# One fused layer on one core: block 0's first u ahead of h_1's moments, fd_hi casts and x differences moved, one output's scaling split in two

## The chip, the cores and the metric

One core of one Trainium2 chip runs the whole program. The metric is device time in microseconds; lower is better. The engines are PE (matrix products; PEld is its weight load), DVE (vector), ACT (scalar activations), POOL (GpSimd) and SP (which here issues transfers). Each engine runs its own instructions one after the other; semaphores tie the engines together.

## The reference

A batch of 4 x 2048 tokens of 256 features passes an attention-like layer without softmax, and then a gated feed-forward layer with integer weights. Both are followed by a layer norm without weights.

```python
Q, K, V = x @ W_q.T, x @ W_k.T, x @ W_v.T          # 256 features
mask = where(i >= j, decay ** (i - j), 0)          # inside chunks of 32 tokens
O = (Q K^T * mask) V                               # chunk by chunk
a = (sigmoid(x @ W_g.T) * O) @ W_o.T + x
h = layernorm(x + a)
f = (silu(h @ wg.T) * (h @ wu.T)) @ wd.T           # 768 hidden, int weights / 127
out = layernorm(h + f)
```

## The kernel before

The 8192 tokens are cut into 16 blocks of 512 (TB). Each block passes an attention stage and a feed-forward stage; the loop over b (0 to 13, from L1088 on) does the feed-forward stage of block b, the scores and values of block n = b + 2, and the token projections (gate, y, v) of block m = b + 3, with their products interleaved on PE. Blocks 0 and 1 have their attention in a prologue ahead of the loop, and blocks 14 and 15 have their feed-forward stage behind it. The iteration b = 13 is the last attention block: there is no block m (the name `more` is false), and its feed-forward products stand alone beside the scores and the output projection of block 15.

Precision comes from splitting operands. A token tile x becomes x_hi (ACT, scaled by TOP), x_lo (POOL, the rest) and x_gap (DVE, a difference made by `gaps()` in `token_parts`, L473); the weights likewise. A projection is then three products in `three` (L520): hi by hi and lo by lo first, then ACT multiplies the bank by WHOLE in place (L527), then gap by gap is added to the same bank, and `finish` takes it away. So PE cannot start the gap products (p_v, p_y, p_g, p_o) before ACT has scaled that bank. The hidden values u are split into u_hi (fp32r, ACT, L898) and u_lo (f16, POOL, L899), h into hT_hi and hT_lo.

`ffn_up` makes one chunk of 128 hidden features: 16 products into the banks fg and fu, s = silu(fg) on ACT (L882), u = fu * s on DVE (L893), then u_hi on ACT and u_lo on POOL. With `held=True` the part from u on is handed back as `multiply`, to be called after other work has been put between. There are six chunks, 0 to 5, for each block. The down projection (`project_back`, or the chunkwise form in `ffn_down` for b = 13) needs all u_hi and u_lo of a block; the chunkwise form does the terms of chunks 0 to 3 first, then the p_o gap products of block 15, then the rest.

The weights fg, fu and fd come as int32 tiles. `integers` (L272) hands back a function that casts one of the two forms, hi or lo, in three pieces on ACT (L282). For fd, the hi form is cast at b = 0 behind `look_up(range(4, n_pieces))`, which takes maxima of the integer tiles on DVE; the lo form is cast between s and u of chunks 4 and 5 of b = 0 by `up_with_cast`.

The layer norm of h takes its mean and variance with bn_stats and bn_aggr on DVE (`moments`, L332 and L333, eight instructions a block). Most blocks take the root on ACT; h_0, h_1, the last h and the last outputs use a chain on POOL (`iterated_scale_and_shift`: a power at L408, then short steps). `normalize` applies scale and shift with four ACT instructions (L420). From block 1 on h goes through `move_h`: four 32x32 transposes on DVE (sq), then 16 transfers on the SP queue (hT), then the split into hT_hi (ACT) and hT_lo (POOL). Outputs are normalized by the same `normalize` one iteration later and stored from SP.

What sets the order: the code writes it out by hand. `in_turn` and `in_steady_turn` pin an instruction behind everything traced on its engine before it. Instructions without it, such as those of the POOL chain, may be placed earlier by the scheduler when their inputs are ready. In the prologue, before the change, the order around h_1 is:

```python
    x_parts, x_gaps = token_parts(xTs[3], "x_3")
    scales_h = iterated_scale_and_shift(out_rest(), of_h, "h_1")
    x_gaps()
    ahead = yT, v, sg
```

`out_rest()` issues the p_o gap products of block 1, the two additions that make h_1 (L784), and the moments. Chunk 0 of block 0 comes after all of that, as the first thing in the loop.

Of the kernel before, what the change touches and what calls it, by code (L numbers as in the profile page):

```python
# [59 lines left out]
NG = TB // P  # L60
# [16 lines left out]
def kernel(  # L77
# [249 lines left out]
    def moments(r, name, groups=range(NG), order=free, mv=None):  # L327

        mv = no_moments(name) if mv is None else mv
        for g in groups:  # L330
            st = small.tile([P, 6], F32, tag="st", name=f"st_{name}_{g}")
            order(nc.vector.bn_stats(st, r[:, g, :]))  # L332
            order(nc.vector.bn_aggr(mv[:, g, :], st))  # L333
        return mv
# [33 lines left out]
    of_h, of_out = (HALF, H_UP), (H_UP, 1.0)  # L368
# [19 lines left out]
    def iterated_scale_and_shift(mv, kind, name):  # L388
        on_r, on_dst = kind

        def column(tag):
            return small.tile([P, NG], F32, tag=tag, bufs=2, name=f"{tag}_{name}")

        def times(out, a, b):
            nc.gpsimd.tensor_tensor(out, a, b, ALU.mult)

        def line(out, a, slope, at_0):
            nc.gpsimd.tensor_scalar(out, a, slope, at_0, ALU.mult, ALU.add)

        v, y, t, minus, shift = map(  # L400
            column, ("v", "y", "t", "minus_mean", "term")
        )
        in_turn(
            nc.vector.tensor_scalar(
                v, mv[:, :, 1], 1 / on_dst**2, EPS * (on_r / on_dst) ** 2, ALU.mult, ALU.add
            )
        )
        nc.gpsimd.tensor_tensor(y, v, half, ALU.pow)  # L408
        nc.gpsimd.tensor_scalar(minus, mv[:, :, 0], -1.0, None, ALU.mult)
        times(t, y, y)  # L410
        times(t, t, v)
        line(t, t, -0.5, 1.5)
        times(y, y, t)
        times(shift, y, minus)
        return y, shift
# [216 lines left out]
    def attn_scores(b, yT):  # L632
        xt = xTs.pop(b)
        ps = bank(f"ps_{b}")[:, : NG * CHUNK].rearrange("p (g c) -> p g c", c=CHUNK)
        for g in range(NG):
            score_products(ps[:, g, :], xt[:, :, g * P :], yT[:, :, g * P :], in_turn)
        sTs.append(sTs.pop(0))
        masked(sTs[-1], ps, range(NG), in_steady_turn)
        return sTs[-1]
# [136 lines left out]
    def split_out(b, go_parts):  # L776

        xn = xns.pop(b)
        r = norm.tile([P, NG, D], F32, tag="h", name=f"h_{b}")
        per = TB // D  # L780

        def finish(i, pb):
            gs = slice(i * per, (i + 1) * per)
            in_steady_turn(nc.vector.tensor_tensor(flat(r, gs), pb, flat(xn, gs), ALU.add))  # L784

        others = three(f"o_{b}", token_major(w_parts["wo"], go_parts), finish)

        def rest():
            others()
            return moments(r, f"a{b}", order=in_turn)  # L790

        return r, rest
# [24 lines left out]
    def move_h(b, h):  # L817

        sq = moved.tile([P, D // SQ, NG, SQ], F32, tag="sq", name=f"sq_{b}")
        for g in range(NG):
            in_turn(
                nc.vector.transpose(
                    sq[:, :, g, :], h[:, g, :].rearrange("p (j f) -> p j f", f=SQ)
                )
            )
        hT = moved.tile([P, KD, NQ, NG * SQ], F32, tag="hT", name=f"hT_{b}")
        for q in range(NQ):  # L830
            for j in range(NQ):
                nc.sync.dma_start(
                    hT[j * SQ : (j + 1) * SQ, :, q, :],
                    sq[q * SQ : (q + 1) * SQ, j::NQ, :, :].rearrange(
                        "p k g t -> p k (g t)"
                    ),
                )
        return hT
# [154 lines left out]
    hs, hTs = {}, {}  # L993
# [10 lines left out]
    x_parts, x_gaps = token_parts(xTs[1], "x_1")  # L1004
# [23 lines left out]
    v_1, rest = split_v(1, x_parts)  # L1028
# [37 lines left out]
    look_up([3])  # L1066
    gate()
    x_parts, x_gaps = token_parts(xTs[3], "x_3")
    scales_h = iterated_scale_and_shift(out_rest(), of_h, "h_1")
    x_gaps()  # L1070
    ahead = yT, v, sg


# [1 line left out]

    scales_out = r_out = None

    def up_now(b, hT, uT, hc):
        ffn_up(b, hT, uT, range(hc, hc + 1))

    def up_with_cast(b, hT, uT, hc, pieces):

        multiply = ffn_up(b, hT, uT, range(hc, hc + 1), held=True)
        if b == 0:
            cast_fd(1, pieces)
        multiply()

    for b in range(NB - 2):  # L1088
        n = b + 2
        m = b + 3  # L1090
        more = m < NB
        xns[n] = load_xn(n)
        hT = hTs.pop(b)
        uT = [], []
        yT, v, sg = ahead
        if b:
            normalize(hs[b + 1], *scales_h)
        up_now(b, hT, uT, 0)
        multiply = ffn_up(b, hT, uT, range(1, 2), held=True)
        if b:  # L1100
            moving = move_h(b + 1, hs[b + 1])
        if more:
            multiply()
        sT = attn_scores(n, yT)
        if not more:
            multiply()
        if m + 1 < NB:
            xTs[m + 1] = load_xT(m + 1)
        multiply = ffn_up(b, hT, uT, range(2, 3), held=True)
        if more:  # L1110
            v_next, v_rest = split_v(m, x_parts)
        multiply()
        if b == 0:
            normalize(hs[b + 1], *scales_h)
            moving = move_h(b + 1, hs[b + 1])
        if more:
            up_now(b, hT, uT, 3)
            v_rest()
            if scales_out is not None:
                normalize(r_before, *scales_out)  # L1120
                store(b - 2, r_before)
        goT = attn_values(n, sT, v, sg)
        if b == 0:
            look_up(range(4, n_pieces))
            cast_fd(0)
        if b == 1:
            count = count_wide()
            n_wide_early = const.tile([1, 1], I32, tag="n_wide_early", name="n_wide_early")
            nc.vector.tensor_copy(n_wide_early, count)
        go_parts, go_gaps = token_parts(goT, f"go_{n}")  # L1130
        if more:
            y_next, y_rest = split_y(m, x_parts)
        else:
            up_now(b, hT, uT, 3)
            normalize(r_before, *scales_out)
            store(b - 2, r_before)
        if not more:
            scales_out = iterated_scale_and_shift(mv_out, of_out, f"out_{b}")
        up_with_cast(b, hT, uT, 4, range(2))
        if more:  # L1140
            go_gaps()
            up_with_cast(b, hT, uT, 5, range(2, 3))
        r_before = r_out
        if more:
            y_rest()
            sg_next, g_rest = split_gate(m, x_parts)
            hs[n], out_rest = split_out(n, go_parts)
            if b:
                hTs[b + 1] = split_h(b + 1, moving)
            g_rest()  # L1150
            mv_h = out_rest()
            if b == 0:
                hTs[b + 1] = split_h(b + 1, moving)
            ahead = y_next, v_next, sg_next
            if m + 1 < NB:
                x_parts, x_gaps = token_parts(xTs[m + 1], f"x_{m + 1}")
            std_h = root_in_turn(mv_h, of_h, f"h_{b}")
            if b:
                mv_before, std_before = mv_out, root_in_turn(mv_out, of_out, f"out_{b}")
            back_to_silu()  # L1160

            def between():
                scales = scale_and_shift(mv_h, std_h, of_h, f"h_{b}")
                if m + 1 < NB:
                    x_gaps()
                return scales

            r_out, mv_out, scales_h = ffn_down(b, uT, hs.pop(b), between)
            if b:
                scales_out = scale_and_shift(mv_before, std_before, of_out, f"out_{b}")  # L1170
        else:
            multiply = ffn_up(b, hT, uT, range(5, KH), held=True)
            hs[n], out_rest = split_out(n, go_parts)
            multiply()
            go_gaps()
            hTs[b + 1] = split_h(b + 1, moving)
            normalize(r_before, *scales_out)
            store(b - 1, r_before)

            def amid():  # L1180
                return iterated_scale_and_shift(out_rest(), (HALF, 1.0), f"h_{n}")

            r_out, mv_out, scales_h = ffn_down(
                b, uT, hs.pop(b), chunkwise=True, amid=amid
            )
            normalize(hs[n], *scales_h)
            scales_out = iterated_scale_and_shift(mv_out, of_out, f"out_{b + 1}")
# [347 lines left out]
```

## Time and profile before

| What | Value |
|---|---|
| three runs | 497.23, 497.33, 497.87 us; median 497.33 |
| the profiled execution | 497.47 us |
| its span, first to last instruction | 495.8 us |
| around the span | 1.67 us |
| granted PE clock, mean | 0.997 |
| one piece of fd_hi on ACT | 627 to 630 ns |
| one normalization of 128x256 on ACT (L420), mean | 590 ns for h |
| bn_stats and bn_aggr of h, mean | 401 and 182 ns |
| an addition for h on DVE (L784), mean | 686 ns |

Times are from the start of the span. A timeline row gives start, length, engine, line, operation, output and inputs, and how many were merged; in brackets, the idle time before it and the instruction that ended it. Merged rows of one engine overlap at their edges, because a PE, ACT or DVE instruction starts before the one ahead of it is recorded as ended. A row of the table of stretches gives the length, then the busy time of PE, PEld, DVE, ACT and POOL with the number of instructions, the granted clock, the share of DMA and its rate. PE's idle time is the measure that counts here, and a PE instruction that starts on time but waits for a second operand looks longer instead of late.

### The profile page before, as it was taken

The numbers are of one execution on the slowest core, as the hardware profiler recorded it, in microseconds if no ns is written. First come the engines' busy times: TensorE is split into PE (matmuls) and PEld (weight loads), VectorE is DVE, ScalarE is ACT, GpSimd is POOL, SyncE is SP. The second block draws the span as 40 slices with busy tenths as digits, with TensorE's granted clock in tenths as the row PEclk, the third lists the DMA queues.
The fourth block names the chain that finished last, engine by engine and source line by source line (L and its number), as shares of the span: only waits on it lengthen the run. The fifth ranks groups of instructions, "written<-read, shape, count | busy, mean of one in ns | idle before, by whom it ended". The sixth has DMA issues, their size and how long they took to land.

```text
span 495.8 us, 12306 instructions
## 1 busy us (share of the span) xinstructions
PE 486.9 (98%) x4760; PEld 382.5 (77%) x4760; DVE 305.1 (62%) x754; ACT 375.4 (76%) x701; POOL 291.1 (59%) x324
## 2 busy tenths in 40 slices
PE   9999999999999999999999999999999999999995
PEld 5787777787977778787787978778787777967674
DVE  4576778474764847557474764847557474766555
ACT  4877697688868778787788868778787787756945
POOL 3835655655745656475655745656475555458664
PEclk9999999999999999999999999999999999999998
DMA  8820213113222231223213222231222211113101
GB/s 261 247 89 7 87 41 88 38 44 81 92 65 65 75 98 44 74 63 93 73 44 84 88 67 63 87 85 44 78 68 84 74 44 42 46 28 102 40 25 66
DMA packets 43324, 37.00 MB, mean 75 GB/s; under 512 B 4864, under 2 KB 39168, under 8 KB 43264
## 3 DMA queue, kind: packets, MB, share of 16 engines
q1 hardware_dynamic: 42144, 35.28, 23.9%
q10 hardware_dynamic: 1120, 0.92, 0.6%
q8 instruction: 38, 0.62, 0.5%
q14 instruction: 22, 0.18, 0.1%
HBM read 20.45 MB, written 8.39 MB: 58 GB/s over the span
## 4 chain that ended last, share of the span: by engine, by line
PE 86%; DVE 5%; ACT 4%; issue 2%; POOL 1%; DVEq 0%; ACTq 0%; POOLq 0%
PE fg L873 15%; PE fu L873 14%; PE fdn L730 13%; PE p_y L486 9%; PE p_g L486 8%; PE p_v L508 8%; PE p_o L508 8%; PE po L684 3%; PE ps L648 2%; PE fdn L947 2%; DVE u L893 1%; ACT s L882 1%; PE pi L193 1%; DVE st_a L332 1%; PE pv L614 1%
## 5 line engine op out<-in xcount | busy, mean ns | idle before, releaser
L899 POOL TENSOR_TENSOR u_lo<-u,u_hi 128x512 f16<-128x512 f32 (+1 forms) x98 | 128.6, 1314 | 86.0 <-ACT u_hi L898 85.3
L893 DVE SCALAR_TENSOR_TENSOR u<-fu,s 128x512 f32<-128x512 f32 (+1 forms) x98 | 66.5, 679 | 106.6 <-ACT s L882 84.0
L898 ACT CAST u_hi<-u 128x512 fp32r<-128x512 f32 (+1 forms) x98 | 59.9, 611 | 64.1 <-DVE u L893 64.0
L873 PE MATMUL fg<-hT_hi,fg_hi 128*128 128x512 f32 (+1 forms) x196 | 71.2, 444 | 0.0
L882 ACT ACTIVATE s<-fg 128x512 f32<-128x512 f32 (+1 forms) x98 | 57.0, 582 | 8.1 <-PE fg L873 8.0
L873 PE MATMUL fu<-hT_hi,fu_hi 128*128 128x512 f32 (+1 forms) x196 | 60.6, 390 | 0.0
L873 PE MATMUL fg<-hT_lo,fg_lo 128*128 128x512 f16 (+1 forms) x196 | 58.1, 378 | 0.0
L873 PE MATMUL fu<-hT_lo,fu_lo 128*128 128x512 f16 (+1 forms) x196 | 57.4, 375 | 0.0
L467 POOL TENSOR_TENSOR go_lo<-goT,go_hi 128x512 fp32r<-128x512 f32 x30 | 37.9, 1285 | 26.7 <-ACT go_hi L466 26.7
L850 POOL TENSOR_TENSOR hT_lo<-hT,hT_hi 128x512 f16<-128x512 f32 x28 | 35.4, 1287 | 23.8 <-ACT hT_hi L849 23.8
L467 POOL TENSOR_TENSOR x_lo<-xT,x_hi 128x512 fp32r<-128x512 f32 x30 | 37.9, 1284 | 14.5 <-ACT x_hi L466 14.5
L730 PE MATMUL fdn<-fd_hi,u_hi 128*128 128x256 f32 x312 | 44.6, 285 | 0.0
L873 PEld LDWEIGHTS fu<-hT_hi,fu_hi 128*128 128x128 f32 x196 | 36.5, 188 | 8.4
L784 DVE TENSOR_TENSOR h<-p_o,x 128x512 f32<-128x512 f32 x30 | 19.3, 686 | 37.4 <-PE p_o L508 35.6
L873 PEld LDWEIGHTS fg<-hT_hi,fg_hi 128*128 128x128 f32 x196 | 34.7, 189 | 9.1
L730 PEld LDWEIGHTS fdn<-fd_hi,u_hi 128*128 128x128 f32 x312 | 38.9, 188 | 0.3
L420 ACT ACTIVATE h<-h,shift_h,scale_h 128x256 f32<-128x256 f32 x52 | 27.0, 590 | 15.9 <-POOL shift_h L383 15.9
L730 PE MATMUL fdn<-fd_lo,u_lo 128*128 128x256 f16 x312 | 38.6, 273 | 0.0
L873 PEld LDWEIGHTS <-fu_lo 128*128 128x128 f16 x196 | 19.2, 98 | 22.2
L730 PEld LDWEIGHTS <-u_lo 128*128 128x128 f16 x312 | 28.4, 98 | 3.9
L873 PEld LDWEIGHTS <-fg_lo 128*128 128x128 f16 x196 | 14.1, 98 | 21.1 <-issue 13.0
L703 DVE SCALAR_TENSOR_TENSOR goT<-sg,po 128x512 f32<-128x512 f32 (+1 forms) x34 | 20.7, 652 | 15.2 <-PE po L684 15.1
(174 smaller groups left out, 1052.9 us busy)
## 6 DMA issues: line engine op xcount, KB each, us to landing
x<-in_x_dram SPq DMA_DIRECT2D x16, 512.0 KB, 4.0
xT<-in_xT_dram SPq DMA_DIRECT2D x15, 512.0 KB, 3.9
hT<-sq SPq DMA_DIRECT2D x224, 32.0 KB, 1.9
out_dram<-r SPq DMA_DIRECT2D x13, 512.0 KB, 3.1
out_dram<-r SPq DMA_DIRECT2D x7, 128.0 KB, 1.7
fg_int<-in_ffn_gT_dram SPq DMA_DIRECT2D x3, 256.0 KB, 7.9
fu_int<-in_ffn_uT_dram SPq DMA_DIRECT2D x3, 256.0 KB, 7.1
fd_int<-in_ffn_dT_dram SPq DMA_DIRECT2D x3, 256.0 KB, 5.9
```

What stands on the lines that cost most here:

```text
L420: nc.scalar.activation(r[:, g, :], r[:, g, :], AF.Identity, bias=shift[:, g : g + 1], scale=scale[:, g : g + 1],)
L467: in_turn(nc.gpsimd.tensor_tensor(lo[:, k, :], t[:, k, :], whole, ALU.subtract))
L486: nc.tensor.matmul(pb, lhsT=a[kind][:, k, i * P : (i + 1) * P], rhs=b[kind][:, k, :], start=kind + k == 0, stop=True, skip_group_check=True,)
L508: nc.tensor.matmul(pb[:, j * D : (j + 1) * D], lhsT=b[kind][:, k, g * P : (g + 1) * P], rhs=a[kind][:, k, :], start=kind + k + j == 0, sto ...
L703: nc.vector.scalar_tensor_tensor(by_pairs(goT)[:, n, r, :], by_pairs(sg)[:, n, r, :], 1.0, po[:, n, :], ALU.add, ALU.mult,)
L730: product = nc.tensor.matmul(pb[:, j * D : (j + 1) * D], lhsT=part[:, g * P : (g + 1) * P], rhs=w, start=(i == 0), stop=(i == len(terms) - 1),
L850: nc.gpsimd.tensor_tensor(in_order[1], whole, in_order[0].bitcast(F32), ALU.subtract)
L873: product = nc.tensor.matmul(pb, lhsT=w[kind][:, dc, hc * P : (hc + 1) * P], rhs=hT[kind][:, dc, cols], start=(kind == kinds[0] and dc == ...
L882: in_turn(nc.scalar.activation(s, pg, AF.Silu, scale=SCALE / H_UP))
L893: nc.vector.scalar_tensor_tensor(u, pu, U_UP / H_UP, s, ALU.mult, ALU.mult)
L898: in_steady_turn(nc.scalar.copy(hi, u))
L899: in_steady_turn(nc.gpsimd.tensor_tensor(lo, u, hi.bitcast(F32), ALU.subtract))
```

## The change

Four things are changed in the order of instructions; nothing is computed differently, and no instruction is added or taken away.

1. `rest` of `split_out` takes a function that it calls between the additions of h and the moments. For block 1, this function is chunk 0 of block 0: its products, s, two pieces of the fd_hi cast, and u, u_hi and u_lo. In the loop chunk 0 is then left out for b = 0.
2. The third piece of fd_hi is cast between s and u of chunk 1 of b = 0. The call of `cast_fd(0)` behind `look_up` is gone. `up_with_cast` takes the form to cast as an argument.
3. `x_gaps()` for x_3 is called behind `attn_scores` of b = 0, and so behind the four mask multiplications on DVE, instead of behind the scales of h_1.
4. At b = 13 the four ACT instructions that normalize the output of block 11 are no longer together behind chunk 3. Groups 0 and 1 come between s and u of chunk 2, and groups 2 and 3 between s and u of chunk 3.

```diff
-        def rest():
+        def rest(between=None):
             others()
+            if between is not None:
+                between()
             return moments(r, f"a{b}", order=in_turn)
...
-    scales_h = iterated_scale_and_shift(out_rest(), of_h, "h_1")
-    x_gaps()
-    ahead = yT, v, sg
...
-    def up_with_cast(b, hT, uT, hc, pieces):
+    def up_with_cast(b, hT, uT, hc, kind, pieces):
 
         multiply = ffn_up(b, hT, uT, range(hc, hc + 1), held=True)
         if b == 0:
-            cast_fd(1, pieces)
+            cast_fd(kind, pieces)
         multiply()
+
+    uT_0 = [], []
+    mv = out_rest(lambda: up_with_cast(0, hTs[0], uT_0, 0, 0, range(2)))
+    scales_h = iterated_scale_and_shift(mv, of_h, "h_1")
+    ahead = yT, v, sg
...
-        uT = [], []
+        uT = ([], []) if b else uT_0
         yT, v, sg = ahead
         if b:
             normalize(hs[b + 1], *scales_h)
-        up_now(b, hT, uT, 0)
+            up_now(b, hT, uT, 0)
         multiply = ffn_up(b, hT, uT, range(1, 2), held=True)
         if b:
             moving = move_h(b + 1, hs[b + 1])
+        else:
+            cast_fd(0, range(2, 3))
         if more:
             multiply()
         sT = attn_scores(n, yT)
+        if b == 0:
+            x_gaps()
         if not more:
             multiply()
...
         multiply = ffn_up(b, hT, uT, range(2, 3), held=True)
         if more:
             v_next, v_rest = split_v(m, x_parts)
+        else:
+            normalize(r_before, *scales_out, range(NG // 2))
         multiply()
...
             look_up(range(4, n_pieces))
-            cast_fd(0)
...
         else:
-            up_now(b, hT, uT, 3)
-            normalize(r_before, *scales_out)
+            multiply = ffn_up(b, hT, uT, range(3, 4), held=True)
+            normalize(r_before, *scales_out, range(NG // 2, NG))
+            multiply()
             store(b - 2, r_before)
         if not more:
             scales_out = iterated_scale_and_shift(mv_out, of_out, f"out_{b}")
-        up_with_cast(b, hT, uT, 4, range(2))
+        up_with_cast(b, hT, uT, 4, 1, range(2))
         if more:
             go_gaps()
-            up_with_cast(b, hT, uT, 5, range(2, 3))
+            up_with_cast(b, hT, uT, 5, 1, range(2, 3))
```

More of the change, by code (lines that the diff above doesn't have):

```diff
@@ L1068, with up_now @@
     x_parts, x_gaps = token_parts(xTs[3], "x_3")
-    scales_h = iterated_scale_and_shift(out_rest(), of_h, "h_1")
-    x_gaps()
+    def up_now(b, hT, uT, hc):
+        ffn_up(b, hT, uT, range(hc, hc + 1))
+    def up_with_cast(b, hT, uT, hc, kind, pieces):
+        multiply = ffn_up(b, hT, uT, range(hc, hc + 1), held=True)
+        if b == 0:
[4 more added lines that the diff above has]
+    scales_h = iterated_scale_and_shift(mv, of_h, "h_1")
     ahead = yT, v, sg
     scales_out = r_out = None
-    def up_now(b, hT, uT, hc):
-        ffn_up(b, hT, uT, range(hc, hc + 1))
-    def up_with_cast(b, hT, uT, hc, pieces):
-        multiply = ffn_up(b, hT, uT, range(hc, hc + 1), held=True)
-        if b == 0:
-            cast_fd(1, pieces)
-        multiply()
     for b in range(NB - 2):
@@ L1104 @@
         sT = attn_scores(n, yT)
+        if b == 0:
+            x_gaps()
         if not more:
@@ L1133 @@
         else:
-            up_now(b, hT, uT, 3)
-            normalize(r_before, *scales_out)
+            multiply = ffn_up(b, hT, uT, range(3, 4), held=True)
+            normalize(r_before, *scales_out, range(NG // 2, NG))
+            multiply()
             store(b - 2, r_before)
```

## The prediction

> **What bounds the kernel now.** I read the page first, then the waits of PE, then a table of stretches cut at the first product of chunk 0 of each block, then the timeline around the two places where PE waits.
>
> ```profile
> span 495.8 us, 12306 instructions
> PE 486.9 (98%) x4760; PEld 382.5 (77%) x4760; DVE 305.1 (62%) x754; ACT 375.4 (76%) x701; POOL 291.1 (59%) x324
> ```
>
> PE is busy for 98% of the span, so only stretches in which PE stands still, or is stretched by a late operand, can be shortened. The waits of PE (us in total, times, longest):
>
> ```profile
> PE p_y L486 <- ACT p_y L527: 1.0, 1, 1.0
> PE fdn L947 <- POOL u_lo L899: 0.7, 1, 0.7
> PE p_v L508 <- ACT p_v L527: 0.2, 1, 0.2
> ```
>
> The stretches (length, then busy time by engine): block 0, block 1, block 2, the last attention block (b = 13), and within that the bank 0 and bank 1 products of its down projection and the p_o gap products.
>
> ```profile
> 45.52:77.28 31.76, 30.57 (x299) 23.37 (x297) 25.80 (x59) 25.51 (x49) 20.03 (x21) 1.00 0.24 68
> 77.28:107.07 29.79, 29.79 (x300) 23.69 (x299) 19.11 (x46) 21.64 (x40) 17.81 (x17) 1.00 0.20 54
> 107.07:136.70 29.63, 29.63 (x298) 23.60 (x297) 18.09 (x45) 23.27 (x43) 17.51 (x19) 1.00 0.25 72
> 433.11:455.27 22.16, 21.45 (x251) 15.87 (x249) 13.68 (x30) 15.77 (x30) 14.99 (x22) 1.00 0.18 49
> 447.80:450.40 2.60, 1.89 (x18) 1.52 (x17) 0.69 (x1) 1.79 (x4) 2.26 (x7) 1.00 0.26 69
> 450.40:452.25 1.85, 1.85 (x19) 1.73 (x17) 1.52 (x3) 1.85 (x5) 1.14 (x2) 1.00 0.78 257
> 452.25:453.52 1.27, 1.27 (x12) 1.08 (x9) 0.61 (x2) 1.27 (x3) 1.27 (x1) 1.00 0.00 0
> ```
>
> Block 0 does the same products as block 2 and takes 31.76 - 29.63 = 2.13 us longer. That is the ceiling of what can be won in block 0. Setting its PE rows beside those of block 2, the lag against block 2 grows by 0.55 up to p_y's first products (around the p_v gap), by 1.27 at the p_y gap, and by 0.3 at the p_g gap. All three follow a scaling by WHOLE on ACT. In the last attention block bank 0 takes 2.60 against 1.85 for bank 1 (0.75 too much), and the p_o gap products 1.27 where the same eight took 427.68 - 426.74 = 0.94 a block earlier (0.33 too much). Why ACT is late in block 0, by the timeline (start, length):
>
> ```profile
> 47.41 0.63 ACT L882 ACTIVATE s<-fg 128x512 f32<-128x512 f32 x1
> 50.41 1.31 DVE L473 SCALAR_TENSOR_TENSOR x_gap<-x_hi,xT 128x512 fp32r<-128x512 f32 x2
> 51.64 0.68 DVE L893 SCALAR_TENSOR_TENSOR u<-fu,s 128x512 f32<-128x512 f32 x1
> 52.35 0.62 ACT L898 CAST u_hi<-u 128x512 fp32r<-128x512 f32 x1 [4.31 <-DVE u L893]
> 56.74 2.08 ACT L420 ACTIVATE h<-h,term_h,y_h 128x256 f32<-128x256 f32 x4
> 61.59 1.67 ACT L282 CAST fd_hi<-fd_int 128x512 fp32r<-128x512 int32 x3
> 64.21 1.07 ACT L527 ACTIVATE p_y<-p_y 128x512 f32<-128x512 f32 x2
> 64.85 1.22 PE L486 MATMUL p_y<-x_gap,m_gap 128*128 128x512 f32 x4 [0.98 <-ACT p_y L527]
> ```
>
> The reader is to see that ACT has s of chunk 0 by 48.04 and then stands for 4.31 us, because DVE does the moments of h_1 (48.08 to 50.29) and both x_gap before the first u. Later the same engine runs without a break from 60.11, with three fd_hi casts in the middle, and PE waits behind it.
>
> **What the Trainium skill says.** "Perfetto Trace Analysis", section "Tensor Engine Instruction", says that ACT, DVE and GpSimd are strict first-in-first-out, and that PE's ends are estimated. The trace agrees: u_hi of chunk 0 blocks s of chunk 1, and I compare PE by starts. "SBUF — State Buffer", section "SBUF: two separate sides", says that a DVE operation with two SBUF inputs and a GpSimd operation lock each other out for a whole instruction. The trace agrees in kind: an x_gap is 684 ns in the median and 1779 ns at most, and the power y_h beside the x_gap of block 0 took 1433 against 1037 ns. "DMA: Bandwidth & Descriptors", section on the anatomy of one DMA, puts a fixed cost of about 2.0 us on a transfer; the hT transfers here land after 1.9.
>
> **Block 0, part by part.** The u of chunk 0 is put ahead of the moments: the two h additions end at 48.16, so u runs from 48.2 to 48.9 instead of 51.64. Moments follow in the same 2.2 us, to 51.0, v_h to 51.2. Two fd_hi casts follow s on ACT: 48.0 to 49.15 (pitch 0.52, last 0.63). They are free, since u needs only s and ACT was idle; cover gone, they would cost 1.15. Then u_hi to 49.75, s of chunk 1 (its products end near 48.9) to 50.3, the third fd_hi to 50.9. u of chunk 1 waits for v_h on DVE: 51.2 to 51.9, u_hi to 52.6, s of chunk 2 to 53.1, p_v scaled by 53.6 and 54.4 (before: 55.8 and 56.3). DVE meanwhile: four masks 51.9 to 53.1, two x_gap to 54.4, u of chunk 2 to 55.1. PE, 0.1 to 0.3 ahead of its old times, asks for the p_v gap at about 55.5, so p_v (54.4) and x_gap (54.4) are both there. The 0.55 goes.
>
> u_hi of chunk 2 ends at 55.7. The scales of h_1 are needed then: the POOL chain took 3.0 us from 50.38 to 53.41, so from 51.2 it ends at 54.2; with the x_gap lock, 54.9. The u_lo of chunk 1 was traced after the chain and pinned behind it, so it cannot delay it. So h_1 is normalized at 55.7 instead of 56.74, 1.0 earlier. From there to p_y ACT has the same list less the fd_hi row, 1.57: p_y runs from 64.21 - 1.0 - 1.57 = 61.6 to 62.7. PE without its waits asks for p_y's gap at 64.85 - 0.98 - 0.55 = 63.3. The 1.27 goes, with 0.6 in hand. p_g at 69.18 becomes 66.7 to 67.7, asked for at 69.81 - 1.82 = 68.0: the 0.3 goes. What is late next is ACT's p_o, 67.7 to 68.8, asked for at 68.9.
>
> Behind that stands h_1's way to hT: 16 transfers on SP from 59.33, 10.3 us of issuing plus 1.9, so landed by about 71; 1.0 earlier is 70, when sg ends on ACT as well. Hence hT_hi, hT_lo, x_lo, the scales of h_2 and s of block 1 all move by about 2.1, as far as PE's chunk 0 (77.28 to 75.2). look_up stays where it was; no load or store passes another on SP or POOL. The fd_int loads were issued at 12.7 to 15.0, long before the casts. Block 0 gives 2.0 of its 2.13 (bounds 0.6 and 2.13).
>
> **Last attention block.** Timeline before:
>
> ```profile
> 446.15 2.08 ACT L420 ACTIVATE r<-r,shift_out,scale_out 128x256 f32<-128x256 f32 x4
> 448.94 2.57 POOL L899 TENSOR_TENSOR u_lo<-u,u_hi 128x512 f16<-128x512 f32 x2
> 450.27 0.39 PE L947 MATMUL fdn<-fd_lo,u_lo 128*128 128x256 f16 x2 [0.71 <-POOL u_lo L899]
> 451.34 1.32 DVE L473 SCALAR_TENSOR_TENSOR go_gap<-go_hi,goT 128x512 fp32r<-128x512 f32 x2
> ```
>
> Half of the four normalizations (1.04) goes before u_hi of chunk 2, half before u_hi of chunk 3. The first pushes u_hi from 441.99 to 442.2, and u_lo and both go_lo on POOL by 0.22. The second pushes u_hi of chunk 3 by 0.2, and frees s of chunk 4 from 448.14 to 446.7, so chunk 5's u and go_gap come some 1.5 earlier. PE's wait, however, is for u_lo of chunk 3, whose u_hi was ready at 446.25: it stood behind the out_13 chain on POOL (446.56 to 448.99), which in turn stood behind go_lo (to 446.46). Nothing in the diff turns this order, so I take the wait to stay and to grow by 0.22, while the 0.33 at the p_o gap goes, and the transposes' wait for h, behind the p_o gap, shrinks by 0.1: net +0.2. Bounds: -0.3 if all of the push arrives, +1.2 if the chain lets u_lo go first.
>
> **Sum.** 2.0 + 0.2 = 2.2. The profiled execution was 497.47 (span 495.8 and 1.67 around it), so 495.3; from the median, 497.33, it is 495.1, which I take.
>
> **Rivals.** (1) u_lo of chunk 3 passes the chain on POOL. For it: it was ready 0.2 before go_lo ended. Against: the order before. It adds 0.75 to 1.0: 494.3. (2) The gain is handed on to block 1: if h_1 is normalized no earlier than 56.74, hT_hi stays at 72.08 and s of chunk 0 in block 1 at 81.24, 6.0 after a chunk start at 75.2 instead of 3.96. Block 1's second p_v scaling ends at 86.64, its products ask near 87.2, so 0.6 of the 2.1 is covered and 1.5 is lost: 497.33 - 0.6 - 0.2 = 496.5, and less loss for half the delay. For it: a DMA path of 12 us that no engine's speed changes. (3) Slower: the moved x_gap now stands on DVE when POOL does u_lo of chunks 0 and 1, and loses the port to both. Free, the second x_gap ends at 54.4; two locks of 1.28 and the chain, slowed to 55.5, put it at 58.2. Then u and u_hi of chunk 2 (1.35), normalization at 59.6, p_y end 59.6 + 6.97 = 66.6 against 65.28 before: 1.3 more wait at p_y, less the 0.2 of the last attention block: 498.4. It decides from a normalization of h_1 later than 56.74 + 1.57 = 58.3. For it: the 1779 ns row. Against: the x_gap beside the chain before took 1.31 for two.
>
> **How the numbers follow.** About 0.2%, 1.0 us, can be told from no change. Forecast 0.56 (494.7 to 495.7), rival 1 0.12, rival 2 0.20 (495.7 to 496.9), rival 3 0.12 (496.9 to 498.8). The range 494.0 to 496.8 leaves out rival 3 and little else. Faster by over 0.2% (below 496.3): 0.56 + 0.12 + 0.13 of rival 2 = 0.81; within: 0.07 of rival 2 and 0.03 of rival 3 = 0.10; slower 0.09.
>
> **What would show it.** Right: block 0 from chunk 0 to chunk 0 takes 29.6 to 29.8, no PE wait at p_y, h_1 normalized near 55.7, the fd_hi casts between 48 and 51. Block 1 longer than 29.8 would be rival 2; x_gap of block 0 longer than 1.0 each, rival 3. In the last attention block, bank 0 still at 2.6 to 2.8 and the p_o gap at 0.94; bank 0 at 1.85 is rival 1. The forecast is wrong if blocks 2 to 12 change at all.

## The result and the profile after

The changed kernel takes 496.79 us in the median of 22 runs, against 497.64 us for the kernel before in 22 runs on the same chips. The ratio is 0.9982, with a 95% interval of 0.9976 to 0.9988: about 0.9 us faster, where 2.2 was forecast. The profiled execution took 496.14 us with a span of 494.6.

The page of the changed kernel, then the waits of PE (us in total, times, longest):

```profile
span 494.6 us, 12306 instructions
PE 485.8 (98%) x4760; PEld 382.8 (77%) x4760; DVE 307.2 (62%) x754; ACT 375.2 (76%) x701; POOL 291.7 (59%) x324
```

```profile
PE p_o L508 <- DVE go_gap L473: 1.0, 1, 1.0
PE pi L193 <- PEq L1531: 1.0, 1, 1.0
PE fdn L949 <- POOL u_lo L901: 0.8, 1, 0.8
```

The waits at p_v and p_y are gone. A new one of 1.0 has come, for a go_gap. The table of stretches of the changed kernel shows where each belongs: block 0, block 1, the last attention block, and in it bank 0, bank 1 and the p_o gap products.

```profile
45.15:74.92 29.77, 29.77 (x299) 23.58 (x297) 25.94 (x59) 25.66 (x49) 20.50 (x21) 1.00 0.26 72
74.92:104.67 29.75, 29.75 (x300) 23.69 (x299) 19.09 (x46) 21.64 (x40) 17.79 (x17) 1.00 0.20 55
430.79:454.04 23.25, 21.47 (x250) 15.88 (x249) 15.26 (x30) 15.63 (x30) 16.32 (x22) 1.00 0.20 58
445.50:448.14 2.64, 1.89 (x19) 1.52 (x17) 0.17 (x1) 1.87 (x4) 2.31 (x7) 1.00 0.30 85
448.14:449.97 1.83, 1.83 (x19) 1.71 (x17) 1.83 (x3) 1.28 (x3) 1.63 (x2) 1.00 0.67 223
449.97:452.29 2.32, 1.29 (x12) 1.09 (x9) 1.65 (x2) 2.32 (x5) 2.32 (x2) 1.00 0.00 0
```

Block 0 fell from 31.76 to 29.77, by 1.99. The last attention block rose from 22.16 to 23.25, by 1.09, nearly all of it in the p_o gap products (1.27 to 2.32). What lies between took 355.83 before and 355.87 after; the tail 40.53 and 40.56. So 1.99 - 1.09 = 0.90 is the effect, and the medians (0.85) agree. The two spans differ by 1.2 and not by 0.9, because chunk 0 of block 0 began at 45.52 in the one and at 45.15 in the other. Scatter of the prologue alone is that large: in two further profiles that share the prologue of the kernel before (e2 and e6 below), chunk 0 began at 46.47 and 46.63, and in the ten profiles with the changed prologue at 45.15 to 46.31.

Block 0 in the timeline of the changed kernel:

```profile
47.50 1.18 ACT L282 CAST fd_hi<-fd_int 128x512 fp32r<-128x512 int32 x2
47.70 0.68 DVE L895 SCALAR_TENSOR_TENSOR u<-fu,s 128x512 f32<-128x512 f32 x1
52.44 1.29 DVE L473 SCALAR_TENSOR_TENSOR x_gap<-x_hi,xT 128x512 fp32r<-128x512 f32 x2
52.49 0.70 POOL L398 TENSOR_SCALAR t_h<-t_h 128x4 f32<-128x4 f32 x1
55.02 2.08 ACT L420 ACTIVATE h<-h,term_h,y_h 128x256 f32<-128x256 f32 x4
60.92 1.07 ACT L527 ACTIVATE p_y<-p_y 128x512 f32<-128x512 f32 x2
62.85 1.09 PE L486 MATMUL p_y<-x_gap,m_gap 128*128 128x512 f32 x4
```

The first u runs right behind s, the casts lie in what was ACT's idle time, and ACT has scaled p_y by 61.99, 0.86 ahead of PE. The last attention block in the timeline of the changed kernel:

```profile
444.29 1.04 POOL L408 TENSOR_TENSOR y_out<-v_out,half 128x4 f32<-128x4 f32 x1
445.81 0.59 ACT L884 ACTIVATE s<-fg 128x512 f32<-128x512 f32 x1
446.67 2.52 POOL L901 TENSOR_TENSOR u_lo<-u,u_hi 128x512 f16<-128x512 f32 x2
447.97 0.69 DVE L895 SCALAR_TENSOR_TENSOR u<-fu,s 128x512 f32<-128x512 f32 x1 [2.72 <-POOL u_lo L901]
448.57 2.85 DVE L473 SCALAR_TENSOR_TENSOR go_gap<-go_hi,goT 128x512 fp32r<-128x512 f32 x2
449.39 1.49 POOL L901 TENSOR_TENSOR u_lo<-u,u_hi 128x512 f16<-128x512 f32 x1 [0.20 <-ACT u_hi L900]
451.48 0.98 PE L508 MATMUL p_o<-wo_gap,go_gap 128*128 128x256 f32 x6 [1.03 <-DVE go_gap L473]
```

s of chunk 5 ends at 446.40, but u of chunk 5 starts at 447.97. The name in brackets says what it waited for: u_lo of chunk 3 on POOL, which ended then. u has two buffers (`work` has bufs=2), so u of chunk 5 takes the buffer of u of chunk 3, and u_lo of chunk 3 still reads it. It stands behind the out_13 chain, whose first step is the y_out above. Both go_gap follow u on DVE, now at the time at which POOL does u_lo of chunks 4 and 5, and they take 2.85 instead of 1.32. PE has all else it needs for the p_o gap products and waits 1.03 for the second go_gap.

### The profile page after: what moved, and what is told of

Read it like the earlier page. It is cut to its first block, busy times and chain, and to the rows that moved or that the text cites. A ratio compares the mean times of both kernels' runs of the same rounds, so it can differ in the third digit from the quotient of the medians.

```text
span 494.6 us, 12306 instructions
## 1 busy us (share of the span) xinstructions
PE 485.8 (98%) x4760; PEld 382.8 (77%) x4760; DVE 307.2 (62%) x754; ACT 375.2 (76%) x701; POOL 291.7 (59%) x324
## 4 chain that ended last, share of the span: by engine, by line
PE 89%; DVE 4%; ACT 3%; POOL 1%; issue 1%; DVEq 0%; ACTq 0%; POOLq 0%
PE fg L875 16%; PE fu L875 15%; PE fdn L730 13%; PE p_y L486 9%; PE p_v L508 9%; PE p_g L486 8%; PE p_o L508 8%; PE po L684 3%; PE ps L648 2%; PE fdn L949 1%; DVE u L895 1%; ACT s L884 1%; PE pi L193 1%; PE pa L763 1%; PE pv L614 1%
```

## The experiments

The ratio is to the kernel before, on the same chip, with its 95% interval. The lengths are those of block 0 (chunk 0 to chunk 0 of block 1) and of the last attention block (chunk 0 to the first product of block 14) in the profile of each run.

| Run | Ratio (interval) | Block 0 | Last attention block |
|---|---|---|---|
| before | 1 | 31.76 | 22.16 |
| after | 0.9982 (0.9976 to 0.9988) | 29.77 | 23.25 |
| e1, no split | 0.9966 (0.9954 to 0.9978) | 29.80 | 22.18 |
| e2, split only | 1.0021 (1.0012 to 1.0029) | 31.74 | 23.28 |
| e3, three buffers of u | 0.9953 (0.9939 to 0.9967) | 29.80 | 22.05 |
| e4, chain behind u_lo | 0.9946 (0.9932 to 0.9961) | 29.77 | 21.55 |
| e5, go_gap first | 0.9963 (0.9950 to 0.9977) | 29.86 | 22.59 |
| e6, casts only | 0.9982 (0.9975 to 0.9989) | 31.13 | 22.18 |
| e7, order only | 0.9978 (0.9969 to 0.9987) | 30.44 | 22.16 |
| e8, no split, chain behind | 0.9962 (0.9949 to 0.9976) | 29.81 | 22.17 |
| e9, gap from PSUM | 0.9958 (0.9943 to 0.9974) | 29.82 | 21.98 |
| e10, chain early | 0.9944 (0.9932 to 0.9956) | 29.78 | 21.13 |
| e11, e4 again | 0.9936 (0.9923 to 0.9948) | 29.83 | 21.56 |

### e1 and e2: the change cut in two

e1 is the changed kernel without the split, e2 the kernel before with the split alone:

```diff
 # e2; e1 is the reverse, in the changed kernel
         if more:
             v_next, v_rest = split_v(m, x_parts)
+        else:
+            normalize(r_before, *scales_out, range(NG // 2))
         multiply()
...
-            up_now(b, hT, uT, 3)
-            normalize(r_before, *scales_out)
+            multiply = ffn_up(b, hT, uT, range(3, 4), held=True)
+            normalize(r_before, *scales_out, range(NG // 2, NG))
+            multiply()
```

> The changed kernel with the four normalizations of b = 13 together again behind chunk 3, as before the change. Theory A (block 0 gave its 2.0 us, and the split in the last attention block gives 1.1 of it back): block 0 takes 29.77 us, the last attention block 22.2 as before instead of 23.25, p_o gap products without a 1.0 wait, and the time is about 2.0 below before, near 495.6 (ratio 0.996). Theory B (the last attention block is longer because it now runs against an earlier prologue and block 0, whatever the order inside it): 23.2 again, time near 496.8 (0.998).

> The kernel before with nothing but the split of the normalizations at b = 13. Theory A: the last attention block takes 23.2 instead of 22.16, u of chunk 5 waits on DVE for u_lo of chunk 3 by 2 to 3 us, both go_gap take over 2.5 us; time about 1.1 above before, 498.7 (ratio 1.002). Theory B: 22.2 and no change, 497.6 (1.000).

e1 took 496.13 us against 497.94 before, e2 498.98 against 497.94. The waits of PE in e2 hold the new row again, which e1 does not have:

```profile
PE p_o L508 <- DVE go_gap L473: 1.0, 1, 1.0
```

In e2 the 1.1 us are back with the prologue and block 0 as they were before, so the split by itself is slower and the block 0 part by itself is faster (1.8 by the medians, 1.96 in block 0). Theory B falls.

### e3: one more buffer for u

```diff
-                u = work.tile([P, n], F32, tag="u", name=f"u_{b}_{hc}")
+                u = work.tile([P, n], F32, tag="u", bufs=3, name=f"u_{b}_{hc}")
```

> The changed kernel with three buffers for u instead of two; the order on every engine is the same. Theory A1 (u of chunk 5 waits for the buffer of u of chunk 3, which u_lo of chunk 3 still reads behind the POOL chain): u of chunk 5 runs right after its s, near 446.5 on the scale of the changed kernel instead of 447.97, go_gap starts near 447.1, and even if it meets u_lo twice the second one ends by 449.9, so the p_o gap products wait 0.3 at most and the time falls by 0.7 to 1.0, to about 496.0. Theory A2 (only the lock between go_gap and u_lo counts, the buffer doesn't): u may be early, but go_gap ends near 451.4 as in the changed kernel, and the time stays at 496.8.

It took 495.42 us. The timeline of e3 (chunk 0 of the last attention block at 431.71, so 0.92 later than in the changed kernel):

```profile
447.42 0.69 DVE L895 SCALAR_TENSOR_TENSOR u<-fu,s 128x512 f32<-128x512 f32 x1 [1.24 <-POOL y_out L395]
448.02 3.10 DVE L473 SCALAR_TENSOR_TENSOR go_gap<-go_hi,goT 128x512 fp32r<-128x512 f32 x2
450.92 1.23 PE L508 MATMUL p_o<-wo_gap,go_gap 128*128 128x256 f32 x8
```

u of chunk 5 starts 15.71 us after chunk 0 instead of 17.18: the buffer was what it waited for. go_gap is no shorter, 3.10 for two, but it begins 1.47 earlier and ends at 19.41 instead of 20.63, as PE asks for it, so the eight products take 1.07 (450.92 to 451.99) instead of 2.32. The block falls by 1.20, where the time was expected to fall by 0.7 to 1.0. A1 holds for the lateness; A2 is right in that the length is a matter of its own.

### e4 and e11: the chain behind u_lo of chunk 3

```diff
-        nc.gpsimd.tensor_tensor(y, v, half, ALU.pow)
+        order(nc.gpsimd.tensor_tensor(y, v, half, ALU.pow))
 # and so for the other POOL steps of the chain, with order=in_turn at b = 13
-            scales_out = iterated_scale_and_shift(mv_out, of_out, f"out_{b}")
+            scales_out = iterated_scale_and_shift(mv_out, of_out, f"out_{b}", in_turn)
```

> The changed kernel with the POOL chain of out_13 pinned behind u_lo of chunk 3, which is the only order that changes. Theory A1: u_lo of chunk 3 runs right after go_lo, u of chunk 5 no longer waits, PE's wait of 0.75 in bank 0 is gone and so is the 1.0 at the p_o gap; the last attention block falls from 23.25 to 21.3 to 21.8 and the time to about 495.0. Theory A2 (the lock): the chain now runs beside go_gap in short steps, so the lock is brief, and most of the 1.0 goes as well, but bank 0 and p_o gap are told apart by the two waits of PE. Theory D (the chain is urgent: scale and shift of out_13 are late for the four normalizations on ACT, and hT_lo behind them): the wait reappears at fg of block 14, and the time stays near 496.8.

> The kernel of e4 once more (the out_13 chain pinned behind u_lo of chunk 3), to stand beside the one with the chain moved early on one chip: ratio to before 0.9945, last attention block 21.55 us, PE wait of 0.34 for u_lo of chunk 5.

e4 took 495.21 us, e11 494.95. The timeline of e4 (chunk 0 at 431.30):

```profile
444.65 1.31 POOL L901 TENSOR_TENSOR u_lo<-u,u_hi 128x512 f16<-128x512 f32 x1
445.90 1.06 POOL L408 TENSOR_TENSOR y_out<-v_out,half 128x4 f32<-128x4 f32 x1
447.62 1.28 DVE L473 SCALAR_TENSOR_TENSOR go_gap<-go_hi,goT 128x512 fp32r<-128x512 f32 x2
447.69 0.66 POOL L398 TENSOR_SCALAR t_out<-t_out 128x4 f32<-128x4 f32 x1
451.77 0.39 PE L949 MATMUL fdn<-fd_lo,u_lo 128*128 128x256 f16 x2 [0.34 <-POOL u_lo L901]
```

Both waits of the changed kernel are gone with one order, as A1 said. go_gap keeps its 1.28, and a short step of the chain pays instead, 0.66 where 0.19 is usual. What is left is a new wait of 0.34 for u_lo of chunk 5, behind the chain. The transposes' wait for h went too: from first transpose to the next chunk 1.06 (458.50 to 459.56) instead of 1.46 (459.55 to 461.01). The stretch behind the last attention block (chunk 0 of block 14 to chunk 0 of block 15) is 0.26 shorter in e4 and e11 than in the changed kernel (19.43 against 19.69). The likely reason is the wait of 0.34 itself, which lies between the p_o gap and the transposes and gives h that time; no run tests it alone. Theory D falls.

### e5: go_gap ahead of u of chunk 5

```diff
             hs[n], out_rest = split_out(n, go_parts)
+            go_gaps()
             multiply()
-            go_gaps()
```

> The changed kernel with the two go_gap of block 15 put ahead of u of chunk 5 on DVE; nothing else moves. Theory A1 (go_gap was late because it stood behind u of chunk 5, which waited for its buffer): on the changed kernel's scale go_gap runs near 445.3 beside the POOL chain and is done by 447.2, u of chunk 5 stays near 448, the p_o gap products take 0.95 to 1.0 without a wait, the last attention block takes 21.8 instead of 23.25 and the time is near 495.4. Theory A2 (two SBUF inputs against POOL cost go_gap its time wherever it stands): the p_o gap still waits about 1.0, time near 496.8.

It took 495.92 us, but the last attention block took 22.59 and not 21.8. The timeline of e5:

```profile
446.32 1.28 DVE L473 SCALAR_TENSOR_TENSOR go_gap<-go_hi,goT 128x512 fp32r<-128x512 f32 x2
446.56 0.51 POOL L395 TENSOR_TENSOR t_out<-y_out 128x4 f32<-128x4 f32 x1
447.14 0.52 POOL L395 TENSOR_TENSOR t_out<-t_out,v_out 128x4 f32<-128x4 f32 x1
449.78 0.39 PE L949 MATMUL fdn<-fd_lo,u_lo 128*128 128x256 f16 x2 [1.38 <-POOL u_lo L901]
451.75 1.19 PE L508 MATMUL p_o<-wo_gap,go_gap 128*128 128x256 f32 x8
```

The p_o gap no longer waits, as A1 said. But go_gap now falls beside the chain, two of its steps take 0.51 and 0.52 instead of 0.20, u_lo of chunk 3 is that much later, and PE's wait in bank 0 goes from 0.75 to 1.38. I had not counted what go_gap does to POOL.

### e9: the lock by itself

```diff
+                if other is not None:
+                    in_turn(nc.vector.scalar_tensor_tensor(
+                        gap[:, k, :], whole, -WHOLE, other, ALU.mult, ALU.add))
+                    continue
...
-            go_gaps()
+            go_gaps(other)      # other: a PSUM bank, filled by one product
```

> The changed kernel, where the two go_gap of block 15 take the difference with a PSUM bank (filled by one extra 128x512 product, some 0.2 us of PE) instead of with goT, so that they read one SBUF operand instead of two: block 15's gap operand is another one. Order and start stay: u of chunk 5 still waits for its buffer and go_gap starts near 17.8 us after chunk 0's first product of b = 13. Lock theory: each go_gap takes 0.7 and both 1.3 instead of 2.85, the last p_o gap operand is there before PE asks, and the last attention block takes 22.3 to 22.6 instead of 23.25, time near 496.0. If go_gap were slow for another reason (a wait on go_hi, on the bank or on the buffer), it stays at 2.8 and the time near 497.0.

The kernel of e9 leaves out block 15's own gap term; only its times are read. It took 495.91 us. The timeline of e9 (chunk 0 at 431.64):

```profile
447.54 2.52 POOL L908 TENSOR_TENSOR u_lo<-u,u_hi 128x512 f16<-128x512 f32 x2
449.45 1.27 DVE L474 SCALAR_TENSOR_TENSOR go_gap<-go_hi,other 128x512 fp32r<-128x512 f32 x2
450.85 1.19 PE L515 MATMUL p_o<-wo_gap,go_gap 128*128 128x256 f32 x8
```

go_gap starts 17.81 after chunk 0, as in the changed kernel (17.78), and u_lo lies beside it as there. It takes 1.27 instead of 2.85, the eight products 1.02 (450.85 to 451.87) instead of 2.32, and the block 21.98 instead of 23.25, which is more than the expected fall to 22.3 to 22.6. The extra product did not show in the block's length: PE asks for u_lo of chunk 3 later and waits 0.44 for it instead of 0.75. So the 1.6 extra are the second SBUF operand against POOL, which is the lock that the Trainium skill names ("SBUF — State Buffer", section "SBUF: two separate sides"), here with its price.

### e8 and e10: the split without the chain, and the chain early

e8 is e4 without the split. e10 keeps the split and moves the chain:

```diff
             normalize(hs[b + 1], *scales_h)
             up_now(b, hT, uT, 0)
+        if not more:
+            scales_next = iterated_scale_and_shift(mv_out, of_out, f"out_{b}")
...
-            scales_out = iterated_scale_and_shift(mv_out, of_out, f"out_{b}")
+            scales_out = scales_next
```

> The block 0 part, the normalizations of b = 13 not split, and the POOL chain of out_13 pinned behind u_lo of chunk 3. Tells what the split is worth once u_lo of chunk 3 is out of the way. Theory A1: PE's wait in bank 0 is gone here as well; chunk 5 comes some 1.5 later on ACT and DVE than with the split, so go_gap or u_lo of chunk 5 are late by 0.5 to 1.0, and the last attention block takes 21.8 to 22.2; time near 495.6, 0.3 to 0.6 above the split one with the chain pinned. Rival: the split is worth nothing with or without the chain in the way, and both are alike, 495.1.

> The changed kernel with the out_13 chain traced behind chunk 0 of b = 13, where POOL stands idle, instead of behind chunk 3. If the chain ahead of u_lo of chunk 3 is what both waits of the last attention block come from: no PE wait in bank 0, u of chunk 5 right behind its s, no wait at the p_o gap, and no late u_lo of chunk 5 either (0.34 with the chain pinned behind u_lo of chunk 3); the last attention block takes 21.1 to 21.4, and the transposes' wait for h is gone: time 494.4 to 494.9. If u_lo of chunks 0 and 1, pushed by 2.4 us, hold up go_lo: a wait at the p_o products, 21.8 or more, 495.3.

e8 took 495.73 us and 22.17 in the block, so by the length of the block the split is worth 0.6 once u_lo of chunk 3 is out of the way. (The intervals of e8 and e4 overlap; those of e8 and e11 just do not.) Without it u of chunk 5 is late because its s is, go_gap with it, and PE waits at the p_o gap. The timeline of e8:

```profile
448.90 0.69 DVE L895 SCALAR_TENSOR_TENSOR u<-fu,s 128x512 f32<-128x512 f32 x1 [1.24 <-ACT s L884]
449.51 1.31 DVE L473 SCALAR_TENSOR_TENSOR go_gap<-go_hi,goT 128x512 fp32r<-128x512 f32 x2
450.36 1.48 PE L508 MATMUL p_o<-wo_gap,go_gap 128*128 128x256 f32 x8 [0.58 <-ACT u_hi L900]
```

The table of waits names ACT here, but u_hi of chunk 5 is no operand of that product; the operand that came then is go_gap (first one ending near 450.2).

e10 has no PE wait left in the block: 21.13, the shortest of all. The timeline of e10 shows u of chunk 5 right behind its s, with only two buffers, and go_gap done before PE asks:

```profile
447.64 0.69 DVE L895 SCALAR_TENSOR_TENSOR u<-fu,s 128x512 f32<-128x512 f32 x1 [1.24 <-ACT s L884]
448.25 1.31 DVE L473 SCALAR_TENSOR_TENSOR go_gap<-go_hi,goT 128x512 fp32r<-128x512 f32 x2
```

Its time, 495.27, misses the 494.4 to 494.9 expected, since the transposes' wait for h stays (1.46, 458.53 to 459.99), the moments of h having moved with PE. By their intervals e10 and e4 can't be told apart. Either beats the changed kernel (their intervals lie below 0.9976, where its own begins), and the kernel before by some 2.8 us.

### e6 and e7: block 0 cut in two

```diff
 # e6: the kernel before, with
-        up_now(b, hT, uT, 0)
+        multiply = ffn_up(b, hT, uT, range(0, 1), held=True)
+        if b == 0:
+            cast_fd(0, range(2))
+        multiply()
...
+            cast_fd(0, range(2, 3))      # behind s of chunk 1, b = 0
...
             look_up(range(4, n_pieces))
-            cast_fd(0)
 # e7: the changed kernel without these lines and without the split
```

> The kernel before with nothing but the fd_hi casts moved: pieces 0 and 1 between s and u of chunk 0 of block 0, piece 2 between s and u of chunk 1, chunk 0 still behind the moments. If the parts of block 0 overlap (either of them takes the wait at the p_y gap away): the p_v part of 0.5 stays, the waits at p_y and p_g go; block 0 takes 30.2 to 30.4 instead of 31.76 and the time is 1.4 to 1.6 below before, near 496.3. If the parts add up (each gives its share of 2.0 and the order gives most): block 0 takes 30.8 to 31.0, time near 496.9.

> The kernel before with chunk 0 of block 0 ahead of the moments and x_gap behind the masks, the fd_hi casts left in their old place and the normalizations of b = 13 not split. If the parts overlap: h_1 is normalized about 1.3 earlier against chunk 0 than before, the p_v part goes, most of the p_y wait goes, 0.3 to 0.7 is left at p_y and p_g; block 0 takes 30.1 to 30.5, time near 496.3. If they add up, with the casts worth more than 1.0: block 0 takes 30.8 or more, time near 497.0.

e6 gives 31.76 - 31.13 = 0.63 in block 0, e7 31.76 - 30.44 = 1.32; together 1.95, against 1.99 for both. So the parts add up. Neither expectation fits in full: e6 lies above both of its ranges, and e7's 30.44 lies in the range that went with an overlap. My theory that either part alone takes most of it is wrong for the casts. The timeline of e6 shows why they give so little alone:

```profile
66.98 1.51 POOL L899 TENSOR_TENSOR u_lo<-u,u_hi 128x512 f16<-128x512 f32 x1 [1.00 <-ACT u_hi L898]
67.26 1.27 DVE L305 TENSOR_SCALAR wide<-top 128x9 f32<-128x9 f32 x1
69.15 0.62 ACT L898 CAST u_hi<-u 128x512 fp32r<-128x512 f32 x1 [1.24 <-DVE u L893]
70.31 1.22 PE L486 MATMUL p_g<-x_gap,wg_gap 128*128 128x512 f32 x4 [0.67 <-ACT p_g L527]
```

The wait at p_y is gone in e6, and a wait at p_g has taken its place. ACT is early, but u of chunk 5 is not: `wide`, nine values a partition, takes 1.27 on DVE beside a u_lo, and u stands behind it; u_hi and p_g stand behind u.

## Why the prediction was wrong

**Block 0: right, in mechanism and size.** 2.0 was forecast and 1.99 came. u at 47.7, casts to 48.7 and 50.2, no wait at the p_v, p_y and p_g gaps beyond 0.1; h_1 normalized 9.87 us after chunk 0 (55.02 - 45.15), where 55.7 - 45.52 = 10.2 was forecast. Block 1 kept its 29.75, so the handing on of rival 2 did not come. Rival 3 did not come either: x_gap took 1.29 for two. It fell between u_lo of chunk 0 (done at 50.58) and u_lo of chunk 1 (from 54.02), beside the POOL chain, and there it was the chain that paid: two of its steps took 0.70 and 0.52 instead of 0.20, and it still ended at 54.07, ahead of the normalization. e6 and e7 bear the sum out, though the prediction did not say how it divides.

**The last attention block: the step that failed.** The prediction counted +0.2 gain, from "so chunk 5's u and go_gap come some 1.5 earlier" and from the 0.33 of stretch at the p_o gap going. Measured was a loss of 1.09. Three things in that sentence were wrong, and the runs show each:

- s of chunk 5 did come 1.9 earlier against chunk 0 (15.02 instead of 16.94), but u did not follow: it had to wait for the buffer of u of chunk 3 (e3: with a third buffer it follows). The prediction had u_lo of chunk 3 late behind the chain, and used it only for PE's wait. It did not ask who else waits for that u_lo, although the waits of DVE before held a row for u behind u_lo. The profile before already set the limit: u_lo of chunk 3 ended near 450.2 there and u of chunk 5 began at 450.73 (below), so 0.5 was to be had and not 1.5.
- So go_gap moved by 0.45 only, from 18.23 to 17.78 after chunk 0. That took it out of a pause of POOL (before, u_lo ended at 451.51 and the next began at 452.22, and go_gap ran from 451.34 to 452.66, mostly ahead of that next u_lo) and into two u_lo. It grew from 1.32 to 2.85 (e9: 1.27 with one SBUF operand).
- Hence the stretch at the p_o gap did not fall by 0.33 but rose by 1.05 (1.27 to 2.32).

The lines of the profile before that the first two points rest on (chunk 0 at 433.11):

```profile
450.05 0.59 ACT L882 ACTIVATE s<-fg 128x512 f32<-128x512 f32 x1
450.73 0.69 DVE L893 SCALAR_TENSOR_TENSOR u<-fu,s 128x512 f32<-128x512 f32 x1 [1.24 <-ACT s L882]
452.22 1.60 POOL L899 TENSOR_TENSOR u_lo<-u,u_hi 128x512 f16<-128x512 f32 x1 [0.71 <-DMA out_dram<-r]
```

The lock was in the prediction, with its numbers, but as the danger of x_gap in block 0; for go_gap in the last block it was not asked. The wait in bank 0 stayed, as forecast, and grew by 0.04 rather than 0.22. The bound of -0.3 for this part was too narrow by 0.8: its price had no term for a go_gap that takes longer. That 496.79 still lies inside the range of 494.0 to 496.8, at its very edge, is luck: that room had been left for rival 2, which did not come.

So the gain of block 0 was there, and more than half of it was given back in one place. Shown are the place (e1, e2), the buffer (e3), the order on POOL behind it (e4, e10), and the lock (e9). The loss at the p_o gap needed both the buffer and the lock: e3 takes away only the one and e9 only the other, and in each PE's wait there is gone.

## What to carry to other kernels

When an instruction is made earlier, follow its output buffer as well as its inputs: with two buffers the third write waits for the slowest reader of the first, wherever that reader stands in its own queue. Then look at what POOL does at the new time of every DVE operation with two SBUF operands; a move of half a microsecond can turn a 0.7 us operation into 1.8. A chain of tiny POOL steps that nobody needs soon should not be left to float ahead of the piece that everybody waits for: pinning it behind that piece made the last attention block 1.70 us shorter than in the changed kernel (e4), and giving it an idle stretch 2.12 (e10).

## What was not expected of the hardware

The lock reaches small operations. `wide`, 128x9 with one SBUF input, took 1.27 us beside a u_lo in e6, and v_out, 128x4, took 1.03 us in the changed kernel beside go_lo, where the same form takes 0.17 elsewhere in that trace; in e10, where POOL stood idle, v_out of the same block took 0.16. (`wide` stands beside a long POOL operation in every trace, so its free time is not known.) It works the other way too: POOL steps of 0.20 took 0.5 to 0.7 beside go_gap (e4, e5) and beside x_gap (the changed kernel). The operation u on DVE, with one operand in PSUM, showed none of it: it took 0.69 at most in every trace, whatever POOL was doing.
